# First projection cut by columns across two stretches, decay coefficients of two layers made in alternating rounds

## Chip, core and metric

The kernel runs on one NeuronCore of a Trainium2 chip, in float32 throughout. The metric is the device time of one execution in microseconds, given as the median of several runs. Engines are called PE (matrix multiply), PEld (its weight loads), DVE (vector), ACT (activations), POOL (GpSimd) and SP (the queue that issues most of the DMAs).

## Reference

A batch of 8 images of 56x56 pixels with 192 channels passes through four residual layers, each behind a group norm with 32 groups. Only the first two layers, L0 and L1, bear on this change. They have one form:

```python
x = x + L(_gn(x))                       # L0, then L1
# inside L, D1 = 576, n = 56:
p = silu(x @ p_w.T + p_b); q = silu(x @ q_w.T + q_b); v = silu(x @ v_w.T + v_b)
sl = 0.95 + 0.05 * clip(slope, 0, 1)
decay = concat([one, sl**idx, one, (sl**idx)[:, ::-1]], axis=1)[0]    # idx = 1..55
a1 = rpe_mlp(rpe_input, t1_...) * decay ; a2 = rpe_mlp(rpe_input, t2_...) * decay
qv = q * v
o1 = toeplitz(qv along the width, a1); o2 = toeplitz(qv along the height, a2)
return (p * (o1 + o2)) @ o_w.T + o_b
```

`rpe_mlp` is a small network from a position to 576 coefficients (32 wide, three hidden layers). `toeplitz` is a convolution along one axis of the image, per channel.

## The kernel before

**Samples and stretches.** Samples are kept in pairs (j, j+4), so that one tile of 128 partitions by 3 holds the 2x192 channels. Four pairs are worked in two halves, j0=0 (pairs 0 and 1) and j0=2 (pairs 2 and 3). For each layer and half there are three generators: `Q` (`tno_qv`: normalise, project to q and v, silu, product, store to the DRAM tensor `qv`), `TZ` (`tno_toeplitz`: the convolution as matmuls, result to the DRAM tensor `L_sum`) and `O` (`tno_out`: projection p, its product with the sum, output projection, residual). TZ of a half reads what Q of that half stored, O reads what TZ stored.

**The order of work.** A function `weave` runs a list of generators, the lane, one after the other, and lets a TZ generator advance beside it in proportion to the lane's planned time (from 4% to 92% of it). The stretches are:

1. Q(0,0) alone, with the group norm statistics of all pairs (`input_stats`, L218) and the decay tables of both layers;
2. Q(0,2) with TZ(0,0) beside it;
3. O(0,0), then Q(1,0), with TZ(0,2);
4. O(0,2), then the first 512 columns of Q(1,2), with TZ(1,0);
5. the other 640 columns of Q(1,2), then O(1,0), with TZ(1,2);
6. O(1,2), and the layers behind.

Stretch 1 is ordered by a list scheduler on every engine. From stretch 2 on, `tc.manual_schedule(engines=ENGINES)` keeps PE, ACT, DVE and POOL in program order; the SP queue is always ordered by the scheduler.

**Q in detail.** The 3136 tokens of a pair are taken in 13 groups of 256 (L240 loads `t6`, three buffers), and each group in strips of 128 tokens, 25 in all. A strip is projected to 1152 columns, in units of 512, 512 and 128. A unit of 512 is 16 matmuls (L263; float32, each shows as two records of 128x256), two adds of the bias on DVE (L272, out of PSUM), one silu on ACT (L301), one product on POOL (L304) and one store from SP (L307, from `t4`, three buffers). The normalisation is six ACT instructions per group (L246). Columns are ordered so that the first 512 make the first 8 of 18 slices of `qv`, the others the rest. For Q(0,0) the first two groups are done one pair at a time, as soon as the statistics of that pair are there (`half_unit`, L284 and L291, the tiles `z0` to `z11`). PSUM holds four buffers of two banks, and a unit of 512 takes two of them.

**TZ in detail.** It takes 9 blocks of 64 channels, each twice, d=0 along the width and d=1 along the height. It loads `q` (L380, L383, two buffers) and the matrices `tm` (L393, from the decay tables `L_tab`); 16 matmuls make one PSUM tile (L406, 32 records), ACT copies it into `ot` (L413, two buffers of four copies), DVE transposes `ot` (L424, L426), POOL adds the transposed half to `s` (L429) and stores `s` (L436, L444). Blocks 0 to 3 need only the first 8 slices of `qv`.

**Decay tables.** `decay_tables` makes for one layer five tiles of powers, one for each 128 of 576 channels (a load of the slope, L145, two DVE instructions, then 6 scalings L152 and 5 squarings L158), and then for two directions a small network (PE L180, DVE L176, L177, L182) and five chunks of coefficients (PE L187, two DVE instructions L194), each stored with four DMAs on SP (L204, two for the last chunk). It yields 5 + 2 x 8 = 21 times. The tiles have two buffers in most cases. In the kernel before, L0's generator runs to its end before L1's begins, and the two share tile names. Beside it, the rows of `qv` behind the last token are zeroed by two DMAs on POOL (L736, 4032 KB each).

The part of `tno_layers` that the change replaces:

```python
for st in stats[2:]:
    for more in st:
        next(first)
        next(decay)
...
lanes = [[(first, QT - 104.0)], [(Q(0, 2), QT)], [(O(0, 0), OT), (Q(1, 0), QT)]]
...
self.weave(lanes[0], decay, lanes[1][0][0], 28.0, 0.0, 0.75)
```

Of the kernel before, what the change touches and what calls it, by code (L numbers as in the profile page):

```python
# [12 lines left out]
F32 = mybir.dt.float32  # L13
# [14 lines left out]
T = H * W  # L28
HALF = [slice(0, 64), slice(64, 128)]
TT = 448  # L30
NT = T // TT
D1 = 576
# [6 lines left out]
def view(ap, offset, dims):  # L39

    return bass.AP(ap.tensor, ap.offset + offset, [ap.ap[0], *dims])


class Net:
# [91 lines left out]
    def decay_tables(self, L, p, tables):  # L136

        nc, inp = self.nc, self.inp
        tv = p.tile([32, 111], F32, name="tv", bufs=1)
        nc.sync.dma_start(tv, inp["tvec"])  # L140
        pows = []
        for c in range(5):
            m = min(128, D1 - 128 * c)
            sl = p.tile([128, 1], F32, name="sl")
# [3 lines left out]
            pw = p.tile([128, 64], F32, name="pw", bufs=5)  # L148
            nc.gpsimd.memset(pw[:m, 0:1], 1.0)
            n = 1  # L150
            while n < 64:
                nc.vector.tensor_scalar(  # L152
                    pw[:m, n : 2 * n], pw[:m, 0:n], sl[:m], None, ALU.mult
                )
                n *= 2
                if n < 64:
                    sq = p.tile([128, 1], F32, name="sl")
                    nc.vector.tensor_mul(sq[:m], sl[:m], sl[:m])  # L158
                    sl = sq
            pows.append(pw)  # L160
            yield 1.0
        for d in range(2):
            t = f"{L}_t{d + 1}"
            w0 = p.tile([32, 2], F32, name="w0")
            nc.sync.dma_start(w0[:, 0:1], inp[f"{t}_w0"])
            nc.sync.dma_start(w0[:, 1:2], inp[f"{t}_b0"])
            ws = p.tile([32, 3, 32], F32, name="ws")
            nc.sync.dma_start(ws, inp[f"{t}_ws"])
            bs = p.tile([32, 3], F32, name="bs")
# [5 lines left out]
            h = p.tile([32, 111], F32, name="h")  # L175
            nc.vector.tensor_scalar(h, tv, w0[:, 0:1], w0[:, 1:2], ALU.mult, ALU.add)  # L176
            nc.vector.tensor_scalar(h, h, 0.0, None, ALU.max)  # L177
            for i in range(3):
                hp = self.bank2()[:32, 0, :111]
                nc.tensor.matmul(hp, ws[:, i, :], h, start=True, stop=True)  # L180
                h = p.tile([32, 111], F32, name="h")
                nc.vector.tensor_scalar(h, hp, bs[:, i : i + 1], 0.0, ALU.add, ALU.max)  # L182
                yield 1.0
            for c in range(5):
                m = min(128, D1 - 128 * c)
                ap = self.bank2()[:, 0, :111]
                nc.tensor.matmul(  # L187
                    ap[:m], wo[:, 128 * c : 128 * c + m], h, start=True, stop=True
                )
                a = p.tile([128, 4 * self.TG + 56], F32, name="a")  # L190
                nc.gpsimd.memset(a[:m, 111:], 0.0)
                back = view(pows[c][:m], 55, [[-1, 55]])
                for lo, hi, dec in ((0, 55, back), (55, 111, pows[c][:m, 0:56])):
                    nc.vector.scalar_tensor_tensor(  # L194
                        view(a[:m], 110 - lo, [[-1, hi - lo]]),
                        ap[:m, lo:hi],
                        bo[:m, c : c + 1],
                        dec,
                        ALU.add,
                        ALU.mult,  # L200
                    )
                for n in range(m // 32):
                    to = tables[d][self.TG * (4 * c + n) : self.TG * (4 * c + n + 1)]
                    nc.sync.dma_start(  # L204
                        to.rearrange("g (c w) -> c g w", w=self.TW),
                        view(a[32 * n : 32 * n + 32], 0, [[4, self.TG], [1, self.TW]]),
                    )
                yield 1.0
# [472 lines left out]
    def tno_layers(self, x0, x1, x2, gn, last):  # L681
# [18 lines left out]
        with ExitStack() as ctx, ExitStack() as wqp:  # L700
# [7 lines left out]
            with tc.tile_pool(name="tab", bufs=2) as tab:  # L708
                stats = [self.input_stats(x0, gn[0], j, tab) for j in range(4)]
                for more in stats[0]:  # L710
                    pass
                first = Q(0, 0, tab)
                next(first)

                for n in range(14):
                    next(first)
                    next(stats[1], None)
                for more in stats[1]:
                    pass
                for n in range(10):  # L720
                    next(first)
                none = tab.tile([1, 512], F32, name="none", bufs=1)
                nc.gpsimd.memset(none, 0.0)
                for t in tables:
                    for d in range(2):
                        nc.gpsimd.dma_start(t[d][D1 // 32 * self.TG :, :512], none)
                decay = (dt for i in range(2) for dt in self.decay_tables(LS[i], tab, tables[i]))
                for st in stats[2:]:
                    for more in st:
                        next(first)  # L730
                        next(decay)
                rows = tab.tile([128, 3, TT], F32, name="x", bufs=7)[:112].rearrange("p k t -> p (k t)")
                nc.gpsimd.memset(rows[:, :512], 0.0)
                for qv in qvs.values():
                    to = qv[:, T:].rearrange("n (p k) e -> p n (k e)", p=112)
                    nc.gpsimd.dma_start(to, view(rows, 0, [[0, D1 // 32], [1, 512]]))  # L736
                lanes = [[(first, QT - 104.0)], [(Q(0, 2), QT)], [(O(0, 0), OT), (Q(1, 0), QT)]]
                parts = [Q(1, 2, None, cols) for cols in ((0, 512), (512, 2 * D1))]
                lanes += [[(O(0, 2), OT), (parts[0], QT * 4 / 9)], [(parts[1], QT * 5 / 9), (O(1, 0), OT)]]
                lanes += [[(O(1, 2, False), OT)]]  # L740
                self.weave(lanes[0], decay, lanes[1][0][0], 28.0, 0.0, 0.75)
            in_order = tc.manual_schedule(engines=ENGINES)
            with tc.tile_pool(name="tz", bufs=1) as self.tz, in_order:
                self.tms = []
                for i in range(2):
                    self.tms.append(self.tz.tile([128, 32 * self.TW], F32, name=f"tm{i}"))
                for n, tz in enumerate((TZ(0, 0), TZ(0, 2), TZ(1, 0), TZ(1, 2))):
                    self.weave(lanes[n + 1], tz, lanes[n + 2][0][0], TZT)
                wqp.close()
            self.weave(lanes[5], **last())  # L750

# [913 lines left out]
```

## Time and profile before

| | us |
|---|---|
| median of 3 runs | 5474.94 (5457.63 to 5475.17) |
| profiled execution | 5488.15 |
| its span, first to last instruction | 5486.4 |
| mean granted PE clock | 0.976 of full |
| PE busy (share of the span) | 5191.3 (95%) |
| DVE, ACT, POOL busy | 2587.1, 2352.7, 1765.1 (47%, 43%, 32%) |
| stretch 1, to the last matmul of Q(0,0) | 0 to 430 |
| stretch 2, to the first matmul of O(0,0) | 430 to 964 |
| HBM traffic | 735.11 MB read, 363.94 MB written |

Times inside the profile are in us from the start of the span. A row of a timeline has start, duration, engine, line, operation, output and input, count, and in brackets the idle time before it and what ended it. A row of waits has the waiting engine and line, the engine and line that it waited for, total us, number of waits and the longest. A row of windows has a stretch, its length, then busy us and instruction records of each engine, the granted PE clock, the share of time that the DMA engines were busy, and GB/s.

### The profile page before, as it was taken

Reading aid. Unit: us, or ns where it says so; the run is one execution under the profiler, and the core shown is the slowest. Engines: PE = TensorE matmul, PEld = TensorE weight load, DVE = VectorE, ACT = ScalarE, POOL = GpSimd, SP = SyncE. Lnnn points to the kernel's source line nnn. Section 1 sums busy time; section 2 is a strip of 40 time slices with the busy share of each in tenths; the row PEclk is TensorE's granted clock in tenths of the full one; section 3 lists DMA queues with packets and bytes.
Section 4 is the critical chain, followed back from the end, with each engine's and each line's share of the span. In section 5 each row is a group of like instructions: output and inputs, shape, how many; then the busy total and the mean of one; then the engine's idle time right before and its main releaser. Section 6 shows DMA issues by size and latency. Waiting matters only on the chain.

```text
span 5486.4 us, 144239 instructions
## 1 busy us (share of the span) xinstructions
PE 5191.3 (95%) x64672; PEld 3825.7 (70%) x64672; DVE 2587.1 (47%) x3990; ACT 2352.7 (43%) x3113; POOL 1765.1 (32%) x1292
## 2 busy tenths in 40 slices
PE   7999898999999999999999899989999999999998
PEld 3776666777777777776777788855665444777776
DVE  6444555455555555554566322422212331566666
ACT  2344454444554454655454322242323333444443
POOL 1334756133664343545443100000001101333333
PEclk9899999999999999999999999999999999999999
DMA  8558997888786999788897666634444222444443
GB/s 285 139 143 259 300 296 261 253 282 271 240 262 172 312 313 318 267 240 278 285 326 251 203 220 233 217 125 155 146 165 120 76 66 52 80 94 107 100 98 72
DMA packets 1042521, 1108.41 MB, mean 202 GB/s; under 512 B 234256, under 2 KB 977680, under 8 KB 1027504
## 3 DMA queue, kind: packets, MB, share of 16 engines
q1 hardware_dynamic: 902960, 846.82, 51.6%
q0 software_dynamic: 38144, 200.99, 9.6%
q10 hardware_dynamic: 100800, 51.38, 3.6%
q8 instruction: 508, 8.32, 0.6%
q14 instruction: 109, 0.89, 0.1%
HBM read 735.11 MB, written 363.94 MB: 200 GB/s over the span
## 4 chain that ended last, share of the span: by engine, by line
PE 48%; DMA 4%; DVE 2%; issue 2%; POOL 1%; ACT 1%; SPq 0%; POOLq 0%; ACTq 0%; DVEq 0%
PE bank L968 6%; PE bank L829 5%; PE bank L1048 5%; PE bank L1242 4%; PE bank L263 3%; PE bank L592 3%; PE bank L1062 3%; PE bank L536 3%; PE bank L1358 2%; PE bank L1272 2%; PE bank L1189 2%; PE bank L1313 2%; PE bank L586 1%; PE bank L1332 1%; PE bank L406 1%
## 5 line engine op out<-in xcount | busy, mean ns | idle before, releaser
L263 PE MATMUL bank<-wq,t 128*128 128x256 f32 (+4 forms) x7680 | 1300.5, 377 | 93.3 <-DVE t L272 48.4
L263 PEld LDWEIGHTS bank<-wq,t 128*128 128x128 f32 (+2 forms) x7680 | 1011.5, 192 | 374.9 <-issue 101.3
L272 DVE TENSOR_TENSOR t<-bank,wq 128x1024 f32<-128x1024 f32 (+3 forms) x480 | 517.6, 1112 | 695.1 <-PE bank L263 544.3
L304 POOL TENSOR_TENSOR t<-t 128x1024 f32<-128x1024 f32 (+2 forms) x288 | 525.4, 1837 | 636.3 <-ACT t L301 390.9
L413 ACT COPY ot<-bank 128x896 f32<-128x896 f32 x576 | 492.8, 910 | 517.0 <-PE bank L406 313.5
L429 POOL TENSOR_TENSOR s<-s,ot 128x1568 f32<-128x1568 f32 x128 | 550.6, 4304 | 188.4 <-DVE ot L426 123.5
L301 ACT ACTIVATE t<-t 128x2048 f32<-128x2048 f32 (+2 forms) x288 | 422.9, 1488 | 377.9 <-DVE t L272 370.6
L406 PE MATMUL bank<-q,tm 56*32 56x224 f32 x18432 | 506.7, 355 | 33.1 <-ACT ot L413 16.3
L406 PEld LDWEIGHTS bank<-q,tm 56*32 56x32 f32 x18432 | 342.5, 106 | 159.8 <-issue 69.5
L122 POOL DMA_DIRECT2D x<-t x112 | 87.0, 777 | 1098.7 <-DVE t L601 1033.6
L560 DVE TENSOR_TENSOR t<-t,bank 128x896 f32<-128x896 f32 x224 | 242.8, 1087 | 398.8 <-ACT bank L555 340.3
L555 ACT ACTIVATE bank<-bank,wo 128x448 f32<-128x448 f32 x448 | 263.1, 606 | 388.0 <-PE bank L545 368.3
L968 PE MATMUL bank<-z,w 128*128 128x448 f32 (+1 forms) x1344 | 413.2, 555 | 3.7 <-ACT h L977 3.7
L536 PE MATMUL bank<-t,wo 128*128 128x224 f32 x1792 | 374.4, 362 | 21.2 <-ACT t L515 10.7
L536 PEld LDWEIGHTS bank<-t,wo 128*128 128x128 f32 x1792 | 336.8, 193 | 51.6 <-issue 28.3
L592 PE MATMUL bank<-t,wo 128*128 128x224 f32 x1792 | 368.9, 359 | 0.0
L592 PEld LDWEIGHTS bank<-t,wo 128*128 128x128 f32 x1792 | 329.9, 190 | 31.2 <-issue 31.2
L829 PEld LDWEIGHTS bank<-xt,cm 113*112 113x112 f32 x3072 | 315.4, 179 | 43.2 <-issue 33.5
L829 PE MATMUL bank<-xt,cm 113*112 113x108 f32 (+2 forms) x3072 | 323.7, 265 | 11.2 <-ACT h L977 6.4
L968 PEld LDWEIGHTS bank<-z,w 128*128 128x128 f32 (+1 forms) x1344 | 182.6, 189 | 208.2 <-issue 197.9
L424 DVE STREAM_TRANSPOSE s<-ot 128x1792 f32<-128x1792 f32 x144 | 292.6, 2033 | 74.4 <-DMA L_sum<-s 37.8
L127 POOL DMA_DIRECT2D x<-x x64 | 36.7, 574 | 844.9 <-DVE x L999 815.2
(149 smaller groups left out, 6961.1 us busy)
## 6 DMA issues: line engine op xcount, KB each, us to landing
q<-qv SPq DMA_DIRECT2D x36, 3584.0 KB
t<-L_sum SPq DMA_DIRECT2D x112, 1008.0 KB
L_sum<-s POOLq DMA_DIRECT2D x256, 392.0 KB, 7.3
qv<-t SPq DMA_DIRECT2D x192, 512.0 KB
cm<-in_L_cm SPq DMA_DIRECT2D x96, 896.0 KB
tm<-L_tab SPq DMA_DIRECT2D x288, 240.0 KB
q<-qv SPq DMA_DIRECT2D x40, 1568.0 KB
q<-qv ACTq DMA_DIRECT2D x32, 1568.0 KB
```

Of the source, the lines that this page charges most:

```text
L263: nc.tensor.matmul(pp[:m, b, 256 * j : 256 * j + k], x[rows, j, 2 if part else b, s : s + m], w[rows, part, c0 + c : c0 + c + k],  start=p ...
L272: nc.vector.tensor_add(z[:m, c : c + k, :], view(pp[:m], 0, [[1, k], [256, 4]]), view(bias[:m], c0 + c, [[1, k], [0, 4]]),)
L301: nc.scalar.activation(z[:m, :n, :], z[:m, :n, :], AF.Silu)
L304: nc.gpsimd.tensor_mul(prod[:m, :k], half[:, :, 0], half[:, :, 1])
L406: nc.tensor.matmul(pt[32 * j : 32 * j + 32, r, hf * 224 : (hf + 1) * 224], tm[rows, at : at + 32], q[rows, :, 4 * c : 4 * c + 4], start=Tr ...
L413: nc.scalar.copy(view(ot, 4 * (g % 4), [[16, 2], [32, 112], [1, 4]]), view(pt, 0, [[512, 2], [4, 112], [1, 4]]),)
L424: nc.vector.transpose(to, of.rearrange("p (i k) -> p i k", k=32))
L429: add.tensor_add(to, to, view(of, 0, [[1, 28], [32, 56]]))
L536: mm(gs[c // 2][:, b, c % 2 * 256 : c % 2 * 256 + N], pw[:, 0, 128 * c : 128 * c + 128], xn[:, b], start=c % 2 == 0, stop=False,)
L592: mm(P[:, b, :N], ow[:, c, 0:128], g[:, 4 * b + c], start=False, stop=c == 3)
L829: nc.tensor.matmul(pc[:, 128 * e + 4 * m0 : 128 * e + 4 * m1], cm[:113, e, k, :], xt[:, m0 - 1 + k : m1 - 1 + k, c + e, :], start=n == 0 a ...
L968: nc.tensor.matmul(phs[c][:, s, :TT], w0[rows, part, at : at + 128], z[rows, Z[2 if part else s], :], start=part == flip, stop=part != flip,)
```

## The change

Q(0,0) becomes two generators. `first` does groups 0 and 1 with all columns, and groups 2 to 12 (21 strips) with columns 0 to 511. `rest` does groups 2 to 12 with columns 512 to 1151; it loads and normalises those groups again. `rest` is put ahead of Q(0,2) in the lane of stretch 2, so that TZ(0,0) starts beside `rest` when only the first 512 columns are stored.

Stretch 1 is now written out as 28 rounds under `manual_schedule`. A round takes a step of the statistics of pairs 2 and 3 (rounds 0 to 13), one strip of `first` (0 to 20) or one unit of `rest` (21 to 27), a step of L0's decay tables (0 to 20) and a step of L1's (7 to 27). The two decay generators have tile names of their own, but for the weights of the small network. The zeroing of `qv` moves into rounds 14 (for j0=0) and 21 (for j0=2). The planned time by which TZ is paced in stretch 2 grows from 298 (Q(0,2) alone) to 412 (`rest` and Q(0,2)).

```diff
-    def tno_qv(self, L, j0, xs, gn, qv, apart=None, cols=(0, 2 * D1)):
+    def tno_qv(self, L, j0, xs, gn, qv, apart=None, cols=(0, 2 * D1), g0=0):
...
-        if j0 == 0:
+        if j0 == 0 and not cols[0]:
...
-        loaded = [load(0)]
+        loaded = [load(g0)]
         yield 0.0
-        loaded.append(load(1))
+        loaded.append(load(g0 + 1))
...
-        for g in range(2 if apart else 0, groups):
+        for g in range(2 if apart else g0, groups):
...
-                first = Q(0, 0, tab)
+                first, rest = Q(0, 0, tab, (0, 512)), Q(0, 0, None, (512, 2 * D1), 2)
...
-                none = tab.tile([1, 512], F32, name="none", bufs=1)
+                none = tab.tile([112, 512], F32, name="none", bufs=1)
...
-                decay = (dt for i in range(2) for dt in self.decay_tables(LS[i], tab, tables[i]))
-                for st in stats[2:]:
-                    for more in st:
-                        next(first)
-                        next(decay)
-                rows = tab.tile([128, 3, TT], F32, name="x", bufs=7)[:112].rearrange("p k t -> p (k t)")
-                nc.gpsimd.memset(rows[:, :512], 0.0)
-                for qv in qvs.values():
-                    to = qv[:, T:].rearrange("n (p k) e -> p n (k e)", p=112)
-                    nc.gpsimd.dma_start(to, view(rows, 0, [[0, D1 // 32], [1, 512]]))
-                lanes = [[(first, QT - 104.0)], [(Q(0, 2), QT)], [(O(0, 0), OT), (Q(1, 0), QT)]]
+                decay = [self.decay_tables(LS[i], tab, tables[i]) for i in range(2)]
+                more = (dt for st in stats[2:] for dt in st)
+                with tc.manual_schedule(engines=ENGINES):
+                    for n in range(28):
+                        next(more, None)
+                        if n == 18:
+                            next(rest)
+                        if next(first, None) is None:
+                            next(rest)
+                        if n < 21:
+                            next(decay[0])
+                        if n >= 7:
+                            next(decay[1])
+                        if n in (14, 21):
+                            qv = qvs[0 if n == 14 else 2]
+                            to = qv[:, T:].rearrange("n (p k) e -> p n (k e)", p=112)
+                            nc.gpsimd.dma_start(to, view(none, 0, [[0, D1 // 32], [1, 512]]))
...
+                lanes = [[(rest, QT * 5 / 9 * 21 / 25 - 25.0), (Q(0, 2), QT)], [(O(0, 0), OT), (Q(1, 0), QT)]]
...
-                self.weave(lanes[0], decay, lanes[1][0][0], 28.0, 0.0, 0.75)
...
-                    self.weave(lanes[n + 1], tz, lanes[n + 2][0][0], TZT)
+                    self.weave(lanes[n], tz, lanes[n + 1][0][0], TZT)
```

In `decay_tables` the tiles `tv`, `sl`, `pw`, `h` and `a` get the layer's name in front; `w0`, `ws`, `bs`, `wo` and `bo` stay shared, with two buffers.

More of the change, by code (lines that the diff above doesn't have):

```diff
@@ L138, in decay_tables @@
         nc, inp = self.nc, self.inp
-        tv = p.tile([32, 111], F32, name="tv", bufs=1)
+        tv = p.tile([32, 111], F32, name=f"{L}tv", bufs=1)
         nc.sync.dma_start(tv, inp["tvec"])
@@ L143, in decay_tables @@
             m = min(128, D1 - 128 * c)
-            sl = p.tile([128, 1], F32, name="sl")
+            sl = p.tile([128, 1], F32, name=f"{L}sl")
             nc.sync.dma_start(sl[:m], inp[f"{L}_slope"][128 * c : 128 * c + m, :])
@@ L147, in decay_tables @@
             nc.vector.tensor_scalar(sl[:m], sl[:m], 1.0 - 0.95, 0.95, ALU.mult, ALU.add)
-            pw = p.tile([128, 64], F32, name="pw", bufs=5)
+            pw = p.tile([128, 64], F32, name=f"{L}pw", bufs=5)
             nc.gpsimd.memset(pw[:m, 0:1], 1.0)
@@ L156, in decay_tables @@
                 if n < 64:
-                    sq = p.tile([128, 1], F32, name="sl")
+                    sq = p.tile([128, 1], F32, name=f"{L}sl")
                     nc.vector.tensor_mul(sq[:m], sl[:m], sl[:m])
@@ L174, in decay_tables @@
             nc.sync.dma_start(bo, inp[f"{t}_bo"])
-            h = p.tile([32, 111], F32, name="h")
+            h = p.tile([32, 111], F32, name=f"{L}h")
             nc.vector.tensor_scalar(h, tv, w0[:, 0:1], w0[:, 1:2], ALU.mult, ALU.add)
@@ L180, in decay_tables @@
                 nc.tensor.matmul(hp, ws[:, i, :], h, start=True, stop=True)
-                h = p.tile([32, 111], F32, name="h")
+                h = p.tile([32, 111], F32, name=f"{L}h")
                 nc.vector.tensor_scalar(h, hp, bs[:, i : i + 1], 0.0, ALU.add, ALU.max)
@@ L189, in decay_tables @@
                 )
-                a = p.tile([128, 4 * self.TG + 56], F32, name="a")
+                a = p.tile([128, 4 * self.TG + 56], F32, name=f"{L}a")
                 nc.gpsimd.memset(a[:m, 111:], 0.0)
@@ L725, in tno_layers @@
                     for d in range(2):
-                        nc.gpsimd.dma_start(t[d][D1 // 32 * self.TG :, :512], none)
-                decay = (dt for i in range(2) for dt in self.decay_tables(LS[i], tab, tables[i]))
-                for st in stats[2:]:
-                    for more in st:
-                        next(first)
-                        next(decay)
-                rows = tab.tile([128, 3, TT], F32, name="x", bufs=7)[:112].rearrange("p k t -> p (k t)")
-                nc.gpsimd.memset(rows[:, :512], 0.0)
-                for qv in qvs.values():
-                    to = qv[:, T:].rearrange("n (p k) e -> p n (k e)", p=112)
-                    nc.gpsimd.dma_start(to, view(rows, 0, [[0, D1 // 32], [1, 512]]))
-                lanes = [[(first, QT - 104.0)], [(Q(0, 2), QT)], [(O(0, 0), OT), (Q(1, 0), QT)]]
+                        nc.gpsimd.dma_start(t[d][D1 // 32 * self.TG :, :512], none[:1])
+                decay = [self.decay_tables(LS[i], tab, tables[i]) for i in range(2)]
[15 more added lines that the diff above has]
+                            nc.gpsimd.dma_start(to, view(none, 0, [[0, D1 // 32], [1, 512]]))
+                    for more in decay:
+                        assert next(more, None) is None
+                lanes = [[(rest, QT * 5 / 9 * 21 / 25 - 25.0), (Q(0, 2), QT)], [(O(0, 0), OT), (Q(1, 0), QT)]]
                 parts = [Q(1, 2, None, cols) for cols in ((0, 512), (512, 2 * D1))]
@@ L747, in tno_layers @@
                 for n, tz in enumerate((TZ(0, 0), TZ(0, 2), TZ(1, 0), TZ(1, 2))):
-                    self.weave(lanes[n + 1], tz, lanes[n + 2][0][0], TZT)
+                    self.weave(lanes[n], tz, lanes[n + 1][0][0], TZT)
                 wqp.close()
-            self.weave(lanes[5], **last())
+            self.weave(lanes[4], **last())
     HB = 32
```

## Prediction, made before the changed kernel was run

> **What bounds the kernel now.** I read the windows of the first stretches first, to see where PE loses time.
>
> ```profile
> core 0: us, PE busy (x) PEld busy (x) DVE busy (x) ACT busy (x) POOL busy (x), PEclk, DMA share, GB/s
> 97.00:430.00 333.00, 307.07 (x1783) 237.06 (x1782) 150.96 (x263) 129.96 (x134) 122.68 (x92) 0.93 0.61 164
> 430.00:964.00 534.00, 465.15 (x6620) 354.92 (x6618) 287.12 (x202) 262.23 (x294) 315.89 (x187) 0.95 0.87 280
> 1400.00:1700.00 300.00, 296.85 (x3559) 231.86 (x3558) 170.62 (x130) 159.63 (x174) 183.65 (x109) 1.00 0.77 250
> 1850.00:2150.00 300.00, 297.99 (x4244) 234.15 (x4238) 171.12 (x211) 154.60 (x244) 131.31 (x87) 1.00 0.97 327
> ```
>
> PE is full in stretches 3 and 4 (last two rows: 99% busy at full clock), and not in stretch 1 behind the first two groups (92%, clock 0.93) nor in stretch 2 (87%, 0.95). Then the waits of stretch 2 (PE from 452 to 960, ACT and POOL from 470 to 940):
>
> ```profile
> PE bank L263 <- ACT ot L413: 26.3, 9, 5.5
> PE bank L263 <- DVE t L272: 14.5, 6, 6.7
> ACT ot L413 <- POOL s L429: 120.0, 14, 16.6
> POOL t L304 <- DMA qv<-t: 98.3, 10, 16.7
> ```
>
> Read from below: POOL's products wait for stores of `qv` to land behind the large `q` loads; POOL is in order, so the adds into `s` come late; ACT finds no free `ot`; PE finds no free bank. TZ is woven too densely for the DMA. The rate of TZ's own matmuls, in stretch 2 and in stretch 4:
>
> ```profile
> 475.00:925.00 450.00, 121.31 (x4480) 84.32 (x4464) 0.97 0.88 288
> 2200.00:2330.00 130.00, 29.48 (x1088) 20.00 (x1088) 1.00 0.83 278
> ```
>
> That is 4480/450 = 10.0 records per us in stretch 2, and 8.4 in the second, which has Q's units beside TZ as well and where PE is busy 127.07 of 130 us. Last, the timeline, for prices and for what stalls stretch 1:
>
> ```profile
> 476.38 5.65 PE L263 MATMUL bank<-wq,t 128*128 128x256 f32 x32
> 485.36 1.74 PE L406 MATMUL bank<-q,tm 56*32 56x224 f32 x64
> ...
> 108.10 1.15 POOL L736 DMA_DIRECT2D qv<-x  x1
> 135.42 3.03 POOL L304 TENSOR_TENSOR t<-z 128x1024 f32<-128x1024 f32 x2 [26.17 <-DMA qv<-t]
> 130.01 3.06 ACT L246 ACTIVATE t<-t,gn 128x256 f32<-128x256 f32 x6 [20.45 <-DMA t<-in_x]
> ...
> 278.65 0.23 DVE L152 TENSOR_SCALAR pw<-pw,sl 128x4 f32<-128x4 f32 x1
> 278.98 2.32 DVE L152 TENSOR_SCALAR pw<-pw,sl 128x8 f32<-128x8 f32 x1
> ...
> 303.03 8.08 SPq L204 DMA_DIRECT2D L_tab<-a  x8
> ```
>
> A unit of 512 is 5.65 us of PE, one of 128 about 1.5 (records run at 30.28/188 = 0.161 us each in a dense piece), a strip 12.8. TZ is 144 PSUM tiles in 72 pairs of 1.65 net, 118 us. The two zeroing DMAs, issued at 97 and 108, kept the DMA engines so busy that the next `t6` load came 20.45 us late.
>
> **What is moved.** The profiled execution took 5488.15 us, 13.2 above the median; the sum is made against it and 13.2 taken off at the end. The columns of `first` cost 21 x 5.65 = 119 us and those of `rest` 21 x 7.15 = 150. Of `rest`, rounds 21 to 27 do four units of 512 and three of 128, 27 us; 123 go to stretch 2. PE's need there: 123 + 320 (Q(0,2), 25 x 12.8) + 118 = 561, against 438 before, which took 534, so 96 us were lost. In stretch 1, from 97 to 430, 269 us of strips and 13 of small matmuls took 333: 51 lost. What is re-done is 11 loads of `t6` and 66 normalisations on ACT (0.59 each): 39 us of an engine that is half idle in stretch 2 (262 of 534), and 8 MB, both priced at nothing there beyond the DMA rate below; if ACT were the late one, they would cost up to 39.
>
> **Stretch 1 after.** Up to the rounds DVE also did powers and statistics of later pairs (busy 61.75 of the 69 us from 28 to 97), which now come later; PE's last 16 half units need 31 us where they took 38.7 (57.92 to 96.65), so the rounds begin near 91. In a round DVE stands in program order: a pair of adds 2.36, three statistics 1.68, a chain of powers. A clean chain took 2.25 (297.41 to 299.65), one that met a product of POOL 4.30 (278.02 to 282.32). I take 3.3, between the two, as POOL has one product of 2.35 in a round. So ten rounds (0 to 4, 7 to 11) are bound by DVE at 7.3, with the pairs of L194 (0.45) 75 us in all, where PE needs 5.65. The chain begins with a load of 128 slopes, and the order of the SP queue shows two of them (rounds 9 and 11) right behind the four stores of coefficients that DVE makes just before: 4 x 0.53 issue and 2.0 to 2.9 from issue to use (287.81 to 289.85, and 293.97 to 297.41 less its issue), in which DVE stands with the adds behind it and PE then runs out of banks. Two times 4.6, 9 us. Rounds 5, 6, 12, 13 are PE's: 6.1 each, 24. The two ends of the statistics stand in line on PE, DVE and ACT: 0.7 + 2.7 + 0.8 + 2.7 + a table load of 1.3, 8 us each, 16. Rounds 14 to 20: 5.65 and two small matmuls, 6.2 each, 43; 21 to 27: 29. SP's eight stores a round in 16 to 19 are 4.2 us at 0.53 but 8.08 in the row above; behind them stand stores of `qv` that have three buffers, so from 0 to 8 more. The zeroing now comes in two parts, at rounds 14 and 21. If each still delays a `t6` load by half of 20.45, three rounds of lead hide it; from 0 to 10 each, I take 5 for all of SP and zeroing. 91 + 75 + 9 + 24 + 16 + 43 + 29 + 5 = 292, where it was 430. The bounds: 270 with clean chains and no waits behind stores, 320 with a collision in each chain and the upper ends.
>
> The collisions are where a rule speaks against this edit. Of 60 scalings in the trace the median is 0.222 us and the longest 3.177, and the long ones lie on a product of POOL. The Trainium skill (SBUF — State Buffer, Who interferes with whom) has the pair of ports that both engines use held for a whole instruction, the other waiting for all of it. By that rule, which the 2.32 beside the 0.23 agrees with, every chain would meet a product, 4.6 for 3.3 in ten rounds, 13 us on top of the sum.
>
> **Stretch 2 after.** First use of `q`: before, the halves were issued at 436.84 and 443.45 and PE stood 5.83 until 461.31. Now the order has the load behind a store that is about 8 us of PE work ahead of the first L406, and the load needs some 18: I take 16 with the clock lost. The end, from 925, lost 15 (6.68, 1.52 and 1.66 and a clock of 0.80 in that slice) and still does, since the last DVE transposes are the same. The rest of the 96 that were lost, some 70, came from density. TZ would have run at 4608/(0.88 x 438) = 12 records per us had PE not waited, and got 10.0. Now it wants 4608/(0.88 x 561) = 9.3, near stretch 4's 8.4, where PE lost 2%. In bytes: what was 146 MB (534 us at 280 GB/s, less start and end) becomes some 165 MB in 561 us, 294 GB/s, below the 327 that stretch 4 bore with PE 99% busy, but that had no POOL products behind it. A line between 8.4 (2%) and 12 (18%) gives 6% at 9.3, 30 us; a limit at 10.0 gives 2%, 10 us. I take 25, bounds 8 and 70. Stretch 2: 561 + 16 + 15 + 25 = 617, ending at 909.
>
> **Sum.** 964 - 909 = 55 us less; nothing later is touched. 5488 - 55 = 5433 for an execution like the profiled one, 5420 for the median, 1.0% faster. (0.5%, 27 us, is about what can be told from no change.)
>
> **Rivals.**
> - *The density is not the cause.* If a POOL product with stores in line behind `q` loads stalls PE whatever the pace, the 70 stay and `rest` brings more products of the same kind. Then 909 + 45 = 954, 10 us less: 5465. For it: `rest` alone has its 35 products and stores, and POOL waits 98 us on them. Against it: in 2200 to 2330, with the same kind of units, PE lost 3 of 130.
> - *The rounds are too tight (slower).* The mechanism is the SP queue in stretch 1. If slopes wait behind stores that wait for POOL not in two rounds but in all ten with powers, at 4.6 each (37 more), and in 14 to 27 each round waits for its stores of coefficients at 1.0 us an issue (8.08 for 6.2, 28 more), then stretch 1 ends at 357. From 347 on it costs more than the forecast gains. With 25 more from a longer stall in stretch 2 the time is 5510. Against it: the queue's order has the slope of most rounds one round ahead.
> - *No stall is left.* As in 1400 to 1700 (PE 99%), the middle loses 5 and the chains are clean: 5420 - 20 - 20 = 5380. The Trainium skill (DMA: Bandwidth & Descriptors, Bandwidth) gives 436 GB/s as the ceiling of the ports; by it 165 MB take under 400 us, and the DMA would bind nothing. No row here comes near it: 327 GB/s is at a share of 0.97.
> - *It does not do what it says.* The order of the built program shows `rest`'s first seven units in the rounds and ten more before the first L406, so it does; 0.
>
> **Chances.** Forecast 0.62, density not the cause 0.16, too tight 0.10, no stall 0.12. The forecast's own bounds (stretch 1 from 270 to 320, middle from 8 to 70, not all at one end) run from 5385 to 5475. Faster by over 0.5% (below 5447.6): 0.54 of the forecast, the whole of no stall, and 0.04 of the first rival, where stretch 1 comes out at its lower bound: 0.70. Within 0.5%: 0.08 of the forecast and 0.11 of the first rival, 0.19. Slower: the second rival and 0.01 of the first, 0.11. The range, 5372 to 5478, takes in the first and third rival and leaves out the second and little else.
>
> **What would show it.** Right: the last matmul of rounds near 292, DVE over 70% busy in rounds 0 to 13; in stretch 2 the wait of ACT for POOL's `s` well under 120, L406 near 9 records per us, PE over 93% busy, O(0,0) starting near 909. Wrong: waits of DVE L146 for slopes in most rounds, SP waits at L204 of several us a round, or a clock and a PE share in stretch 2 as before.

## The result, and the profile after

The changed kernel takes 5454.9 us (median of 14 runs, 5446.93 to 5471.33), the kernel before 5475.06 (14 runs, 5457.63 to 5481.68). The ratio is 0.9969, with a 95% interval from 0.9961 to 0.9976: 13 to 21 us faster, where 55 were forecast. The profiled execution took 5448.52 us, 6.4 below its median, and that of before was 13.2 above its own. So the two profiles differ by 39.63 us, of which 24 appear behind the point up to which the change reaches. The comparison is therefore made at that point, the first matmul of O(0,0) (L536): 964.0 before, 948.3 after, 15.7 us sooner.

The windows of the two stretches after the change, with the columns of the prediction's first fence:

```profile
92.00:228.00 136.00, 102.30 (x523) 79.00 (x521) 88.69 (x237) 52.04 (x61) 36.52 (x31) 0.84 0.56 158
228.00:273.00 45.00, 44.96 (x251) 34.28 (x250) 18.39 (x33) 22.81 (x27) 15.84 (x15) 0.95 0.89 192
273.00:330.00 57.00, 37.44 (x200) 28.79 (x197) 16.40 (x30) 18.04 (x25) 15.35 (x15) 0.76 0.98 242
395.00:900.00 505.00, 485.12 (x6674) 374.37 (x6679) 287.48 (x213) 285.14 (x330) 323.59 (x185) 0.99 0.91 284
```

The first three rows are the rounds 0 to 13, 14 to 20, and 21 to 27. PE is full only in the second. The last row is the body of stretch 2: PE is 96% busy at a clock of 0.99. The body of before (475 to 925) had 396.84 of 450 us, 88%, at 0.97, and the whole stretch 87% at 0.95. The matmuls of TZ (L406) from 395 to 900, and the waits of stretch 2 (330 to 946):

```profile
395.00:900.00 505.00, 120.96 (x4400) 81.71 (x4407) 0.99 0.91 284
```

```profile
POOL t L304 <- DMA qv<-t: 173.7, 26, 30.4
ACT ot L413 <- POOL s L429: 38.7, 8, 7.2
PE bank L406 <- DMA tm<-L_tab: 11.6, 1, 11.6
PE bank L263 <- ACT ot L413: 4.1, 8, 1.9
```

That is 4400/505 = 8.7 records per us. ACT's wait for POOL's adds fell from 120.0 to 38.7 us, and PE's wait for `ot` from 26.3 to 4.1 (at L406, where it was 14.9 in the kernel before, no such wait is left). POOL itself waits longer for its stores (173.7; 98.3 in the window of before), but now without holding up PE.

The timeline of PE in the rounds shows where stretch 1 stood:

```profile
134.33 0.54 PE L180 MATMUL bank<-L0h,ws 32*32 32x111 f32 x2 [8.05 <-issue]
209.87 0.54 PE L180 MATMUL bank<-L1h,ws 32*32 32x111 f32 x2 [9.92 <-DVE L1h L177]
282.97 0.54 PE L180 MATMUL bank<-L1h,ws 32*32 32x111 f32 x2 [9.31 <-issue]
302.75 0.73 PE L187 MATMUL bank<-L1h,wo 32*128 32x111 f32 x2 [3.90 <-DMA wo<-in_L_t_wo]
313.69 7.72 PE L263 MATMUL bank<-wq,t 128*128 128x256 f32 x32 [6.35 <-ACT t L246]
329.45 0.40 PE L187 MATMUL bank<-L1h,wo 32*64 32x111 f32 x2
```

The first three rows are the first matmul of a small network, in rounds 5, 12 and 20. It takes 0.54 us, but PE is kept in program order, so the units behind it wait too. The brackets of two of them name "issue"; DVE's row shows what it was in the first:

```profile
134.02 0.20 DVE L177 TENSOR_SCALAR L0h<-L0h 32x111 f32<-32x111 f32 x1
```

DVE finished the operand at 134.22, and PE went on at 134.33. In round 5 DVE was simply busy until then, without a pause since 113.8. In round 20 it stood, for a memset of POOL that itself waited for a table store to land:

```profile
281.94 0.45 DVE L194 SCALAR_TENSOR_TENSOR L0a<-bank,bo,L0pw 64x55 f32<-64x55 f32 x2 [4.72 <-POOL L0a L191]
```

The last two waits are for DMAs: `wo`, and the `t6` load of `rest`, for which ACT stood 17.97 us:

```profile
288.21 1.15 POOL L743 DMA_DIRECT2D qv<-none  x1
313.04 3.06 ACT L246 ACTIVATE t<-t,gn 128x256 f32<-128x256 f32 x6 [17.97 <-DMA t<-in_x]
```

The second zeroing DMA was issued 25 us before that normalisation, and took 18.4 us to land.

The sum of the prediction, set against both kernels. "Need" is the prediction's own PE time of each stretch at full clock, "lost" is the rest of it:

| us | rounds begin | need 1 | lost 1 | need 2 | lost 2 | O(0,0) begins |
|---|---|---|---|---|---|---|
| before (97: without rounds) | 97 | 282 | 51 | 438 | 96 | 964 |
| forecast | 91 | 159 | 42 | 561 | 56 | 909 |
| after | 92 | 159 | 79 | 561 | 57 | 948 |

Of the 79 in stretch 1, 53 are idle time of PE (238 us less 184.69 busy), and 26 are matmuls that took longer than priced (184.69 less 159). L263 was busy for 164 us where 146 were priced: the unit behind the wait that ends at 313.69 took 7.72 us where the forecast has 5.65, and the granted clock of 92 to 330 is 0.84. The rest is the small matmuls (L79, L180, L187): they were busy for 23 us, some of it beside L263, where 13 were priced. In the kernel before they took 22, so that price was low for both kernels.

### The profile page after: what moved, and what is told of

The parts are those of the page before. It is cut to its first block, busy times and chain, and to the rows that moved or that the text cites. A ratio compares the mean times of both kernels' runs of the same rounds, so it can differ in the third digit from the quotient of the medians.

```text
span 5446.5 us, 144346 instructions
## 1 busy us (share of the span) xinstructions
PE 5166.3 (95%) x64672; PEld 3811.3 (70%) x64672; DVE 2588.6 (48%) x3990; ACT 2384.0 (44%) x3179; POOL 1767.5 (32%) x1291
## 4 chain that ended last, share of the span: by engine, by line
PE 49%; DMA 3%; DVE 2%; issue 1%; ACT 1%; POOL 1%; SPq 1%; ACTq 0%; POOLq 0%; DVEq 0%
PE bank L976 7%; PE bank L837 5%; PE bank L1056 5%; PE bank L1250 4%; PE bank L263 3%; PE bank L592 3%; PE bank L1070 3%; PE bank L536 3%; PE bank L1366 2%; PE bank L1280 2%; PE bank L1197 2%; PE bank L1321 2%; PE bank L586 1%; PE bank L406 1%; PE bank L1340 1%
## 5 line engine op out<-in xcount | busy, mean ns | idle before, releaser
L263 PE MATMUL bank<-wq,t 128*128 128x256 f32 (+4 forms) x7680 | 1289.1, 374 | 73.5 <-DVE t L272 43.7
L263 PEld LDWEIGHTS bank<-wq,t 128*128 128x128 f32 (+2 forms) x7680 | 1004.9, 190 | 351.6 <-issue 92.5
L406 PE MATMUL bank<-q,tm 56*32 56x224 f32 x18432 | 505.1, 354 | 18.7 <-DMA tm<-L_tab 11.6
L406 PEld LDWEIGHTS bank<-q,tm 56*32 56x32 f32 x18432 | 340.2, 106 | 145.3 <-issue 84.1
L536 PE MATMUL bank<-t,wo 128*128 128x224 f32 x1792 | 372.0, 361 | 21.4 <-ACT t L515 10.2
L536 PEld LDWEIGHTS bank<-t,wo 128*128 128x128 f32 x1792 | 334.9, 192 | 51.0 <-issue 30.2
L592 PEld LDWEIGHTS bank<-t,wo 128*128 128x128 f32 x1792 | 329.9, 190 | 31.2 <-issue 31.2
```

The costliest lines, as they stand in the source:

```text
L263: nc.tensor.matmul(pp[:m, b, 256 * j : 256 * j + k], x[rows, j, 2 if part else b, s : s + m], w[rows, part, c0 + c : c0 + c + k],  start=p ...
L406: nc.tensor.matmul(pt[32 * j : 32 * j + 32, r, hf * 224 : (hf + 1) * 224], tm[rows, at : at + 32], q[rows, :, 4 * c : 4 * c + 4], start=Tr ...
L536: mm(gs[c // 2][:, b, c % 2 * 256 : c % 2 * 256 + N], pw[:, 0, 128 * c : 128 * c + 128], xn[:, b], start=c % 2 == 0, stop=False,)
L592: mm(P[:, b, :N], ow[:, c, 0:128], g[:, 4 * b + c], start=False, stop=c == 3)
```

## Experiments

Theory 1: stretch 2 pays as forecast, since TZ is less dense, and the rest of the forecast was lost in the rounds of stretch 1. All ratios below are to the kernel before, with 95% intervals. The changed kernel has 0.9969; a difference of 0.001 is 5.5 us.

**Density.** TZ(0,0) is paced in stretch 2 as densely as before: it starts only at 28.4% of the lane's planned time, and so runs beside Q(0,2) alone.

```diff
-                    self.weave(lanes[n], tz, lanes[n + 1][0][0], TZT)
+                    self.weave(lanes[n], tz, lanes[n + 1][0][0], TZT, *((0.284,) if n == 0 else ()))
```

> The changed kernel with TZ(0,0) paced over 262 planned us of its lane (from 28.4% to 92%) in place of 363, so beside Q(0,2) alone and as dense as in the kernel before. If density is what PE lost in stretch 2 before: the stretch grows from 616 us by 40 to 70, ACT waits over 100 us for POOL's adds into s (38.7 in the changed kernel), total 25 to 55 us over the changed kernel, so slower than the kernel before too. If density is not the cause (rival): within 10 us of the changed kernel.

Measured: 1.0018 (1.0008 to 1.0027), 27 us above the changed kernel; O(0,0) begins at 976.3, 28 later. Stretch 2 grew by 30 us, less than the 40 to 70 expected. The waits of its stretch 2 (452 to 946) are those of the kernel before:

```profile
ACT ot L413 <- POOL s L429: 110.0, 15, 11.7
PE bank L263 <- ACT ot L413: 29.8, 10, 5.7
```

With the density goes the whole gain. The rival "the density is not the cause" falls.

**The zeroing earlier.** The two DMAs in rounds 6 and 10 in place of 14 and 21.

```diff
-                        if n in (14, 21):
-                            qv = qvs[0 if n == 14 else 2]
+                        if n in (6, 10):
+                            qv = qvs[0 if n == 6 else 2]
```

> The changed kernel with the two zeroing DMAs in rounds 6 and 10 in place of 14 and 21. If the zeroing in round 21 is what held the t6 and wo loads in rounds 21 to 27: ACT's wait of 17.97 us before L246 and PE's waits of 6.35 and 3.90 go, the rounds end 8 to 13 us earlier, total 6 to 13 us lower. If the many small table stores are what fills the DMA engines there (rival): less than 4 us, or a loss of up to 10 where the zeroing now delays loads in rounds 6 to 12.

Measured: 0.9931 (0.9919 to 0.9944), some 21 us below the changed kernel, more than expected. The timeline:

```profile
282.90 8.55 PE L263 MATMUL bank<-wq,t 128*128 128x256 f32 x32 [1.03 <-ACT t L246]
298.69 3.06 ACT L246 ACTIVATE t<-t,gn 128x256 f32<-128x256 f32 x6 [3.09 <-DMA t<-in_x]
315.52 0.40 PE L187 MATMUL bank<-L1h,wo 32*64 32x111 f32 x2
```

ACT's 17.97 became 3.09, the rounds end at 315.9 (329.9 after the change), and O(0,0) begins at 934.0. SP issued the two `t6` loads from 290.90 on, where the changed kernel had issued them from 300.56 on. Rounds 21 to 27 took 37 us where they had taken 57; the wait at L180 of round 20, which falls into that time, shrank from 9.31 to 2.44. Rounds 0 to 20 became 5 us longer: PE's wait at L180 in round 12 grew from 9.92 to 13.96, and DVE's waits for L1's slopes from 10.9 to 18.2.

**Three buffers for the coefficients `a`.**

```diff
-                a = p.tile([128, 4 * self.TG + 56], F32, name=f"{L}a")
+                a = p.tile([128, 4 * self.TG + 56], F32, name=f"{L}a", bufs=3)
```

> The changed kernel with three buffers for each layer's coefficient tile a in place of two. If DVE standing for table stores to land (13.4 us at L194 and 4.7 for POOL's memset behind it) is what PE lost at round 20 (9.31 us): 6 to 10 us lower. If the DMA engines' fill itself is the limit (rival): under 3 us, as the stores land no sooner and the wait moves to the loads of wo and t6.

Measured: 0.9962 (0.995 to 0.9975), no difference that can be told; O(0,0) begins at 949.1. The wait at L180 in round 20 fell from 9.31 to 2.22 us, and the next one, for `t6`, grew from 6.35 to 12.91: a wait moved.

**All slopes first.** The five loads of a layer's slopes stand at the start of its generator, ahead of all table stores.

```diff
+        slopes = p.tile([128, 5], F32, name=f"{L}slopes", bufs=1)
+        for c in range(5):
+            m = min(128, D1 - 128 * c)
+            nc.sync.dma_start(slopes[:m, c : c + 1], inp[f"{L}_slope"][128 * c : 128 * c + m, :])
...
-            nc.sync.dma_start(sl[:m], inp[f"{L}_slope"][128 * c : 128 * c + m, :])
-            nc.vector.tensor_scalar(sl[:m], sl[:m], 0.0, 1.0, ALU.max, ALU.min)
+            nc.vector.tensor_scalar(sl[:m], slopes[:m, c : c + 1], 0.0, 1.0, ALU.max, ALU.min)
```

> The changed kernel with all five slope loads of a layer issued at the start of its table generator. If the slopes behind the table stores cost what was forecast (DVE waits of 5.23 and 5.66 us in rounds 9 and 11, PE idle 5.51 and 9.92): no wait of DVE at L146 and 7 to 12 us lower. If DVE's work in the rounds sets the pace anyway (rival): 2 us or less.

Measured: 0.9934 (0.9921 to 0.9948), some 19 us below the changed kernel, more than the 7 to 12 expected. DVE waits for no slope, the waits at L180 in rounds 5 and 12 shrink to 4.31 and 6.36, rounds 0 to 20 end 10 us sooner and the last round 13 us sooner (316.9). PE still waits 10.64 us for the `t6` load near 301.

**The first h earlier.** The two DVE instructions of each network's first hidden layer, with their loads, are issued at the end of the step before.

```diff
+        def start(d):
+            w0 = p.tile([32, 2], F32, name="w0")
+            nc.sync.dma_start(w0[:, 0:1], inp[f"{L}_t{d + 1}_w0"])
+            nc.sync.dma_start(w0[:, 1:2], inp[f"{L}_t{d + 1}_b0"])
+            h = p.tile([32, 111], F32, name=f"{L}h")
+            nc.vector.tensor_scalar(h, tv, w0[:, 0:1], w0[:, 1:2], ALU.mult, ALU.add)
+            nc.vector.tensor_scalar(h, h, 0.0, None, ALU.max)
+            return h
...
             pows.append(pw)
+            if c == 4:
+                h = start(0)
             yield 1.0
...
+                if (d, c) == (0, 4):
+                    h = start(1)
                 yield 1.0
```

> The changed kernel, with one thing moved: the first two DVE instructions of each small network (its first hidden layer, L176 and L177) and the two loads that they need are issued one step earlier, at the end of the last step of powers or of the last chunk of the direction before; so the matmul at L180 of rounds 5, 12, 13 and 20 finds its operand made a round ahead. Theory 1 (PE stands in its own order at L180, behind a first h that DVE makes only after the adds of the same round, and these waits of 8.05, 9.92, 2.18 and 9.31 us are part of the 38 that stretch 1 lost): the four waits go, part of them comes back at the DVE waits for slopes, and O(0,0) starts some 12 to 25 us sooner, near 928; the time is 12 to 25 lower than the changed kernel's. Rival (the waits only show a DVE that is behind with its adds, and PE would stand at L263 for a bank instead): 0 to 5 lower, with the same microseconds at PE bank L263 <- DVE t L272.

Measured: 0.9963 (0.9951 to 0.9976), 3 us below the changed kernel, within the intervals, where theory 1 had 12 to 25. The rounds end 6.6 us sooner (323.3) and O(0,0) begins 5.9 sooner. The waits at L180 did not all go: the one at round 20 fell to 1.06 us, but those in rounds 5 and 12 only to 6.32 and 5.93, since DVE is behind there by its own work and by the slopes (without the waits for slopes too, in the next run, they are 2.57 and 1.95). And PE now waited 18.4 us for `t6` loads, 14.02 of it at one place, where it had waited 6.3. Most of what was taken away came back, at the wait that the zeroing makes.

**Three of them together** (zeroing, slopes, first h).

> The changed kernel with three edits: the zeroing in rounds 6 and 10, all slopes loaded at the start of each layer's generator, and the first h of each small network made a step earlier. Theory 1 (three separate losses of stretch 1: the load of t6 behind the zeroing and table stores, slopes behind table stores, PE in order at L180): they add up as far as PE's own need allows. Stretch 1 then ends near 285 to 292, where the changed kernel's ended at 330, and the time is 36 to 45 lower than the changed kernel's, near 0.989 of the kernel before. Rival (the edits of the zeroing and of the slopes each mend the same wait, that of ACT's normalisation for t6, and the rest is DVE's backlog): 18 to 25 lower, near 0.993, stretch 1 ending near 308.

Measured: 0.9935 (0.9922 to 0.9948). That is the rival's number, but not its cause. Rounds 0 to 20 ended 17 us sooner, so the edits do add up there, but then:

```profile
265.03 1.23 SPq L213 DMA_DIRECT2D L_tab<-L1a  x2
266.31 0.55 SPq L144 DMA_DIRECT2D w<-in_L_t_w  x1
...
268.31 0.64 SPq L180 DMA_DIRECT2D ws<-in_L_t_ws  x1
```

```profile
271.98 0.54 PE L189 MATMUL bank<-L1h,ws 32*32 32x111 f32 x2 [15.59 <-DMA ws<-in_L_t_ws]
```

The first fence is the SP queue, the second PE. The loads of the last network's small weights stand behind table stores, where the changed kernel had issued `ws` at 236.59. SP's order is the scheduler's, and the edit moved them. The rounds ended at 308.8, after a new wait.

**Zeroing and slopes only.**

> The changed kernel with two edits: the zeroing in rounds 6 and 10, and all slopes loaded at the start of each layer's generator. Alone they left the end of rounds 0 to 20 at 278.7 and 263.3 (273.3 in the changed kernel) and took 37 and 54 us for rounds 21 to 27 (57). Theory 1 (two losses at two places): 263 + 37, so the rounds end near 300 and the time is 25 to 32 below the changed kernel's, near 0.991 of the kernel before. Rival (the place of one load in SP's order decides: here the weights of the last small network, ws and bs, stand behind all table stores of round 20, where the changed kernel issued them at 236.6): PE waits 10 us or more at L180 near 270, the rounds end near 310 as with three edits (308.8), and the time is 18 to 22 below the changed kernel's, near 0.9935.

Measured: 0.9945 (0.9933 to 0.9957), 13 us below the changed kernel, less than even the rival had (18 to 22). The rival's cause did come: the same loads stood behind the stores, PE waited 16.20 us at L180 until 279.64, and the rounds ended at 312.0.

**Weights of their own.** The kernel of three edits, with `w0`, `ws` and `bs` in tiles of each layer's own (names with the layer in front), loaded for both directions at the start of its generator. The second network's first h also moves ahead of the last chunk's coefficients.

```diff
+        small = []
+        for d in range(2):
+            t = f"{L}_t{d + 1}"
+            w0 = p.tile([32, 2], F32, name=f"{L}w0")
...
+            ws = p.tile([32, 3, 32], F32, name=f"{L}ws")
+            nc.sync.dma_start(ws, inp[f"{t}_ws"])
...
+            small.append((w0, ws, bs))
```

> The kernel of three edits (zeroing in rounds 6 and 10, slopes first, first h of each small network a step earlier), and the small weights (w0, ws, bs) of both directions in tiles of each layer's own, loaded at the start of its generator, so that no load of them stands behind table stores in SP's queue. With three edits the rounds ended at 308.8, after a wait of PE of 15.59 us for ws at 272. Theory 1: this wait goes, rounds 21 to 27 take some 37 as with the zeroing moved alone, the rounds end near 293 to 297 (292 was forecast for the changed kernel), and the time is 32 to 40 below the changed kernel's, near 0.9895 of the kernel before. Rival (rounds 21 to 27 are bound by table stores in the DMA engines, whatever the order): the wait goes over to ACT's t6 or to L194's buffers, the rounds end at 305 or later, and the time is within 5 us of the three edits', near 0.9935.

Measured: 5431.68 us, 0.9916 (0.99 to 0.9931), 29 us below the changed kernel (32 to 40 were expected) and the lowest ratio of all. Its rounds:

```profile
92.00:301.00 209.00, 181.76 (x971) 139.44 (x968) 129.27 (x299) 93.81 (x114) 69.85 (x63) 0.90 0.84 217
```

PE is idle for 27 us of the rounds, where it was for 53. They end at 301.3 (not at 293 to 297), and O(0,0) begins at 924.3. Of the 38 us that stretch 1 had lost against the forecast, 28.5 are back.

**The split without the rounds.** The decay tables one layer after the other, all of stretch 1 ordered by the scheduler; the code of `tno_layers` is that of the kernel before, but for these lines, and `tno_qv` is that of the change:

```diff
-                first = Q(0, 0, tab)
+                first, rest = Q(0, 0, tab, (0, 512)), Q(0, 0, None, (512, 2 * D1), 2)
...
-                lanes = [[(first, QT - 104.0)], [(Q(0, 2), QT)], [(O(0, 0), OT), (Q(1, 0), QT)]]
+                lanes = [[(first, 7 * 5.3)], [(rest, QT * 5 / 9 * 21 / 25), (Q(0, 2), QT)], [(O(0, 0), OT), (Q(1, 0), QT)]]
```

> The column split without the rounds: first (512 columns) and the decay tables of both layers one after the other, ordered by the scheduler as in the kernel before, the zeroing at the place it had before; rest (640 columns, all 21 strips) and Q(0,2) in stretch 2 with TZ(0,0) beside them. PE needs 132 us in stretch 1 behind the first two groups and 150 + 320 + 118 = 588 in stretch 2. Theory 1 (the gain is all in stretch 2's lower density, the rounds lose 38 us): if the scheduler fits the tables beside the shorter stretch 1, that ends near 260 to 300 and O(0,0) starts near 905 to 945, so the time is 0 to 45 lower than the changed kernel's. Rival (42 steps of tables in a row do not fit beside 21 strips; the interleaved rounds are what makes the split possible): stretch 1 ends at 330 or later, O(0,0) starts after 975, and the time is 25 us or more above the changed kernel's.

Measured: 1.0022 (1.0012 to 1.0032), 29 us above the changed kernel; O(0,0) begins at 980.5. The rival is right in that the tables do not fit, though stretch 1 ends sooner than it said. The last strip of `first` ends near 316, with 132 us of need from 96 on, so 88 are lost. PE's longest waits:

```profile
261.07 0.73 PE L187 MATMUL bank<-h,wo 32*128 32x111 f32 x2 [15.84 <-DMA wo<-in_L_t_wo]
297.60 2.02 PE L187 MATMUL bank<-h,wo 32*128 32x111 f32 x8 [14.16 <-DMA wo<-in_L_t_wo]
334.48 5.76 PE L263 MATMUL bank<-wq,t 128*128 128x256 f32 x18 [18.30 <-ACT t L246]
```

Two are networks that wait for their weights, and one is the `t6` wait again, on the first strip of `rest`. Stretch 2 lost 664 - 588 = 76 us, that wait included.

**The rounds without the split.** Q(0,0) with all its columns, 28 of its units in the rounds, 35 after them, then stretch 2 as before.

```diff
-                        if n == 18:
-                            next(rest)
-                        if next(first, None) is None:
-                            next(rest)
+                        next(first)
...
-                lanes = [[(rest, QT * 5 / 9 * 21 / 25 - 25.0), (Q(0, 2), QT)], [(O(0, 0), OT), (Q(1, 0), QT)]]
+                    second = Q(0, 2)
+                    self.weave([(first, 35 * 4.0)], None, second)
+                lanes = [[(second, QT)], [(O(0, 0), OT), (Q(1, 0), QT)]]
```

> The interleaved rounds without the split: Q(0,0) with all columns, 28 of its units in the 28 rounds, the other 35 after them, then stretch 2 as in the kernel before (Q(0,2) alone beside TZ(0,0), with the pace of before). Theory 1 (rounds lose PE time, about 79 us in all beside 146 + 13 of need, and the gain came from the split's lower density): the last matmul of Q(0,0) comes near 440 to 455, 10 to 25 after the kernel before; stretch 2 takes 534 as before; the time is 10 to 25 above the kernel before, ratio 1.002 to 1.005. Rival (the rounds are a gain of their own, as the forecast had them: 41 us lost in place of 51): ends near 415 to 420, the time is 10 to 15 below the kernel before, ratio 0.997 to 0.998.

Measured: 1.0059 (1.0045 to 1.0072), 32 us above the kernel before, a larger loss than theory 1 expected. The rounds:

```profile
92.00:318.00 226.00, 167.79 (x878) 130.81 (x875) 110.67 (x294) 60.59 (x60) 59.09 (x64) 0.80 0.66 163
```

Nine strips and one unit are 121 us, 134 with the small matmuls, so the rounds lose 92 of 226 us, and the stall of stretch 2 is there as before: ACT waits 116.0 us for POOL's adds (120.0). O(0,0) begins at 995.8, 31.8 later than before.

Each part alone loses (12 and 32 us), and together they gain 17. With the tables one after the other the split lost 88 us in stretch 1, and the rounds cost PE time that only the lower density pays for.

| kernel | rounds end | O(0,0) begins | against before | ratio less 1, in us of 5475 |
|---|---|---|---|---|
| changed | 329.9 | 948.3 | -15.7 | -17 |
| TZ dense | 327.9 | 976.3 | +12.3 | +10 |
| zeroing early | 315.9 | 934.0 | -30.0 | -38 |
| three buffers of `a` | 327.4 | 949.1 | -14.9 | -21 |
| slopes first | 316.9 | 933.7 | -30.3 | -36 |
| first h early | 323.3 | 942.4 | -21.6 | -20 |
| three edits | 308.8 | 927.8 | -36.2 | -36 |
| zeroing and slopes | 312.0 | 932.5 | -31.5 | -30 |
| own weights | 301.3 | 924.3 | -39.7 | -46 |
| split only | none | 980.5 | +16.5 | +12 |
| rounds only | 317.6 | 995.8 | +31.8 | +32 |

One row of one profile, the start of the next unchanged stage, gives the measured difference to within 8 us each time.

## Why the prediction was right and wrong

**Right: stretch 2.** 617 us were forecast and 618 taken. The parts fit too: PE idle for 20 of the 505 us of the body (25 for the middle), 8.7 records per us (near 9), PE at 96% (over 93%), ACT's wait 38.7 (well under 120). The first L406 came after 11.65 us of idle time (16, with the clock lost), but there the size was luck: the load that came last was `tm`, out of the tables, and not `q`, by which it had been worked out. The repeated loads and normalisations of `rest`, priced at nothing, cost PE 3.2 us of waits for ACT in 330 to 946.

**Right: the start, and rounds 14 to 20.** The rounds began at 92.5 (91 forecast), and 14 to 20 took 45 us (43).

**Wrong: the rounds.** The sum has 201 us for them (292 less 91). They took 238, and this is where the forecast gain went. Three steps failed.

- *"29 + 5" for rounds 21 to 27 was 57 us.* The failed step is "three rounds of lead hide it": the zeroing at round 21 was priced by half of an earlier delay and hidden by a lead of rounds, but the `t6` load was 17.97 us late for ACT. PE was idle there for 20 us: 9.31 at L180 of round 20, 3.90 for `wo`, 6.35 behind the `t6` load. Moving the zeroing alone brought these rounds to 37, with 3.5 of idle time.
- *Rounds 0 to 13, 124 forecast, were 136.* The order of DVE was written down, and the order of PE was not: L180 waits for an h that DVE makes behind the adds of the same round, so PE can't run ahead with the next strip. PE stood there for 8.05, 9.92 and 2.18 us in rounds 5, 12 and 13. Not all of that is on top of the forecast, which had DVE's pace and two waits for slopes in its sum, and both hold h up too. These two came as forecast, in rounds 9 and 11, with 5.23 and 5.66 us for 4.6 each. What PE's order alone cost shows in the run with the first h earlier: the last L79 of these rounds ends at 223.2 there, 5 us sooner than in the changed kernel (228.5). DVE was busy for 65% of the time (over 70% was the sign).
- *The price of PE's work.* All units were priced at 5.65 us, and the small matmuls at 13 in all. In the rounds L263 took 164 us for 146, at a granted clock of 0.84, and the small matmuls 23: 184.69 us of busy PE for a need of 159.

**The collisions.** DVE's chain met a product of POOL in 4 of 10 chains, each time with one instruction of 1.88 to 2.33 us that takes 0.15 to 0.24 in a clean chain:

```profile
161.73 2.33 DVE L152 TENSOR_SCALAR L1pw<-L1pw,L1sl 128x32 f32<-128x32 f32 x1
...
169.91 2.39 POOL L304 TENSOR_TENSOR t<-t 128x1024 f32<-128x1024 f32 x1 [5.88 <-ACT t L301]
169.99 2.33 DVE L158 TENSOR_TENSOR L1sl<-L1sl 128x1 f32<-128x1 f32 x1
```

The row of POOL is the product that the last row met. So a chain cost 2.25 plus 0.4 x 2.1, or 3.1, where 3.3 was taken. The Trainium skill (SBUF — State Buffer, Who interferes with whom) has a two-input DVE instruction, too, held up by a GpSimd instruction that reads; by that rule L158 collides as L152 does, and the last row agrees. That every chain would meet a product, priced at 13 us on top, did not happen.

**The rivals.** "The density is not the cause" fell with the dense kernel. "The rounds are too tight" named SP's queue: slopes waited in three rounds, not in ten. But it came more than half way: stretch 1 ended at 330, between the forecast's 292 and this rival's 357, by waits of another kind for the most part. "No stall is left" did not come.

What stays open: nine us of stretch 1 in the best kernel (301 for 292), how the 12 us of rounds 0 to 13 divide between PE's order and matmuls that took longer than priced, and why stretch 2 of the best kernel took 623 us where the changed kernel's took 618. Of the 55 us, 40 were to come from stretch 2 and came (96 lost became 57); the other 15, from stretch 1, came out as a loss of 23.

## What to carry to other kernels

When a schedule is written out by hand, write down the order of every engine and queue, the fullest one too: here a matmul of half a microsecond in PE's order held up all units behind it for as long as DVE was behind. Do not count on a lead in rounds to hide a large DMA: here one that was issued 25 us ahead still made a load late, and placed earlier it gave back 20 us there and cost 5 in the rounds before. Where several waits stand close together, take them away together: here single edits gave back up to all of their gain at the next wait, and an edit that moves one load can make a new one.

## What the runs showed of the hardware

The DMA engines were full in the last rounds, where the tables are stored, at a low rate. A window of 10 us of the changed kernel, at the place of the table stores, and the DMA's packets in 250 to 290:

```profile
280.00:290.00 10.00, 7.03 (x28) 5.44 (x30) 1.21 (x5) 2.17 (x5) 3.88 (x4) 0.64 1.21 195
```

```profile
DMA packets 24096, 7.70 MB, mean 193 GB/s; under 512 B 18536, under 2 KB 24059, under 8 KB 24093
```

The share is over 1 at 195 GB/s, where 327 GB/s had a share of 0.97 in stretch 4; three packets in four are under 512 bytes. The forecast priced table stores by their issue on SP alone. The Trainium skill (DMA: Bandwidth & Descriptors, Specifications) gives 512 bytes as the least size of a transfer for full rate; these rows agree with it.

The profile names "issue" as releaser for waits that end 0.1 us after another engine's result. Such a row (134.33 and 282.97 above) is read together with the rows of the engine that makes the operand.
